# A two-layer attention kernel: one PSUM bank per head for scores and exponentials, whole sums per key tile, preparation without a bank of its own

## The chip, the cores and the metric

The kernel runs on one core of a Trainium2 chip. The metric is the device time of one execution in microseconds; the time before is the median of three runs. The engines are named as the profile names them: PE is TensorE's matmul stream and PEld its weight loads, DVE is VectorE, ACT is ScalarE, POOL is GpSimd, SP is SyncE, which here issues DMAs.

## The reference, cut to what matters

The input is 2048 tokens of 256 features. Two transformer layers follow each other, each an attention and an MLP with the same MLP weights. The first attention has 16 query heads, 4 key heads, biases and rotary positions; the second has 16 of each and neither biases nor rotation.

```
scores = einsum("bthd,bshd->bhts", q, k) * scale      # head size 16
scores = where(causal, scores, -inf)
probs  = softmax(scores, axis=-1)                     # maximum, exponential, sum, division
x = x + einsum("bhts,bshd->bthd", probs, v).reshape(B, S, 256) @ Wo.T + bo
x = x + ((tanh-gelu of (n @ Wg.T)) * (n @ Wu.T)) @ Wd.T      # n = layernorm(x), 2048 features
```

Everything is 32-bit floating point; the MLP weights arrive as 4-bit codes with scales.

## The kernel before, in words

The tokens are cut into 4 blocks of 512 queries (`NB`, `TB`), each of 4 tiles of 128 (`NT`). A unit of attention is one block b and one group g of four heads, 16 units per layer, run in order by `Attention.run` (L848). A unit has nk = 4(b+1) key tiles of 128 keys, and each key tile has two steps, one for each pair of heads (p = 0, 1).

For every query the maximum over its keys is needed before the exponentials. `max_steps` (L659) makes it for the next unit: a maxima step writes the scores of 128 queries against up to 512 keys for two heads (L670) into a pair of PSUM banks, and DVE reduces both banks at once (L682). At the end `gather` and `turn` (L711, L717) put the negated maxima, as three bf16 parts, into `mT`.

`value_steps` (L724) makes the current unit. `pair` (L750) writes, for two heads r = 0, 1, the negated maxima by a bf16 matmul (L758) and on top of them keys times queries (L763) into one pair of banks, and ACT takes one exponential over both banks (L775) into a buffer `e` (four of them). `values` (L729) multiplies the exponentials of the key tile before with the values, four heads side by side in 32 output columns of the array each (L743), and adds into the bank `av`. It is called twice for a key tile, after each pair, for half of the queries each time; where 256 queries or fewer are left (the last two of the four diagonal key tiles) the first call does all. The 17th column of the values is one, so that the same sum gives the softmax's divisor. `end` copies the sums out (L790), `divide` turns and divides them (L797 to L807).

On diagonal key tiles a mask is added by small matmuls (`add_mask`, L639). This and the reading that follows it are put on a list (`owed`) and done when `settle` (L650) is next called: by the next `pair` or `values`, or, if a maxima mask is on the list, by the next maxima step.

The order on every engine is written out by hand: `weave` (L42) puts side steps between main steps evenly, so that after each pair's scores come the maxima steps of the next unit and the preparation of the next block (norms, turns, projections) and, in the first attention, of the unpacking of the MLP weights, and then the sums (the second part of a step's tuple). The first three steps of a unit take maxima only, the last three take no side steps. In the last unit of a layer there are no maxima. `cut` and `holding` (L67, L74) keep a preparation whose scores bank is still to be read (`plain`, `high`, L539, L543) from being split between units.

PSUM has eight banks. `ps_s` (L121) hands out three pairs of banks in turn, to maxima steps and to exponential pairs alike, and to `features` in the MLP (L930); `ps_av` is one bank, and `ps_m` (L127) is one bank for everything else: turns of the input (L464), projections (L498), values (L565), turned maxima (L711), division (L797), output projection (L837), the MLP's turns (L910) and half of its second product (L959). A buffer that is handed out again makes PE wait for the engine that read it last.

In the second attention a projection is split into a high part that ACT rounds (L545) and a rest that DVE subtracts (L553); both go to DRAM by DMAs that SP issues (L552, L556) and come back in other layouts as `qT` (SP, L631) and `kT` (GpSimd's queue, L618).

## Time and profile before

| what | value |
|---|---|
| time, median of 3 runs | 1888.08 us (1885.3 to 1889.78) |
| the profiled execution's own time | 1890.76 us |
| its span | 1888.9 us |
| PE busy | 1766.7 us, 94% |
| DVE busy | 1123.3 us, 59% |
| ACT busy | 805.2 us, 43% |
| POOL busy | 239.0 us, 13% |
| mean granted clock of TensorE | 0.982 |

The profile is of one execution. Busy time of PE is not time at its peak: matmuls overlap, and their ends are modelled. In a timeline a row is a run of equal instructions on one engine, with start and duration in us; a bracket tells how long the engine sat idle before it and which engine's instruction ended that. In a group row come line, engine, operation, output and inputs by name, shapes, count, then busy us, mean ns of one, and idle time with its releasers. A 32-bit matmul appears as two records, its two passes. PE's groups of attention are L758, L763, L670, L743 and the masks L645; the MLP's are L934 and L959.

### The profile page before, as it was taken

What the parts mean: (1) busy time and instruction counts of PE and PEld (TensorE: products, weight loads), DVE (VectorE), ACT (ScalarE), POOL (GpSimd) and SP (SyncE); (2) the same over time, 40 slices, a digit from 0 to 9 for tenths busy, and PEclk for the clock granted to TensorE, in tenths of its full rate; (3) what the DMA queues carried; (4) which work ended last, traced back from release to release, by engine and by line L of the source; (5) the groups of instructions that cost most, each with busy time, mean ns of one, the idle gap of its engine ahead of it and who ended that gap; (6) DMA issues with size and microseconds to landing.
All of it is one profiled execution on the core that took longest, in us unless ns stands there. A gap on an engine that the chain in (4) does not pass through costs nothing. (4 is left out here: it accounts for less than half of the span.)

```text
span 1888.9 us, 31839 instructions
## 1 busy us (share of the span) xinstructions
PE 1766.7 (94%) x13452; PEld 928.5 (49%) x13452; DVE 1123.3 (59%) x1676; ACT 805.2 (43%) x1069; POOL 239.0 (13%) x437
## 2 busy tenths in 40 slices
PE   5788889999999999999998898999999999999999
PEld 3344444444444456656564444444444444756656
DVE  4567687778786253544445667766877715363442
ACT  1334455555667531222213355556566662131221
POOL 4111321210001011112101010010000001011110
PEclk8889999999999999999998999999999999999999
DMA  4421310310101100001303232041000010000000
GB/s 100 108 60 37 68 52 23 63 35 24 35 24 35 45 6 1 1 0 42 81 1 74 62 72 54 12 90 33 15 13 2 2 46 1 11 1 11 7 6 12
DMA packets 42271, 64.24 MB, mean 34 GB/s; under 512 B 13840, under 2 KB 20880, under 8 KB 41872
## 3 DMA queue, kind: packets, MB, share of 16 engines
q1 hardware_dynamic: 33488, 45.93, 8.2%
q0 software_dynamic: 7680, 15.74, 5.0%
q8 instruction: 106, 1.74, 0.4%
q10 hardware_dynamic: 960, 0.52, 0.1%
q14 instruction: 37, 0.30, 0.1%
HBM read 44.24 MB, written 17.83 MB: 33 GB/s over the span
## 5 line engine op out<-in xcount | busy, mean ns | idle before, releaser
L682 DVE TENSOR_REDUCE mx<-ps_s 128x2 f32<-128x1024 f32 (+3 forms) x640 | 658.2, 1060 | 221.0 <-PE ps_s L645 116.0
L775 ACT ACTIVATE e<-ps_s 128x1024 f32<-128x1024 f32 (+3 forms) x640 | 571.3, 897 | 422.6 <-PE ps_s L763 244.8
L743 PE MATMUL ps_av<-e,v 128*32 128x256 f32 (+1 forms) x4608 | 365.2, 384 | 3.4 <-ACT e L775 3.4
L763 PE MATMUL ps_s<-qT,kT 64*128 64x512 f32 (+3 forms) x1280 | 341.7, 527 | 0.0
L670 PE MATMUL ps_s<-kT,qT 64*128 64x512 f32 (+3 forms) x1280 | 269.2, 423 | 52.3 <-DVE mx L682 22.8
L758 PE MATMUL ps_s<-mT,sel 64*128 64x512 bf16 (+3 forms) x1280 | 232.7, 358 | 27.3 <-ACT mT L717 10.1
L934 PE MATMUL ps_s<-xnT,wg 128*128 128x512 f32 x512 | 242.1, 595 | 0.0
L934 PE MATMUL ps_s<-xnT,wu 128*128 128x512 f32 x512 | 240.6, 592 | 0.0
L670 PEld LDWEIGHTS ps_s<-kT,qT 64*128 64x128 f32 x1280 | 130.1, 188 | 161.6 <-ACT e L775 66.5
L758 PEld LDWEIGHTS <-sel 64*128 64x128 bf16 x1280 | 75.0, 93 | 251.2 <-issue 242.3
L942 DVE TENSOR_TENSOR t<-ps_s,t 128x512 f32<-128x512 f32 x128 | 88.1, 688 | 164.5 <-POOL t L941 162.7
L940 ACT ACTIVATE t<-ps_s 128x512 f32<-128x512 f32 x128 | 76.2, 595 | 251.8 <-PE ps_s L934 251.3
L943 ACT ACTIVATE t<-t 128x512 f32<-128x512 f32 x128 | 80.6, 629 | 200.7 <-DVE t L942 200.7
L934 PEld LDWEIGHTS ps_s<-xnT,wu 128*128 128x128 f32 x512 | 97.3, 190 | 122.7 <-issue 122.7
L941 POOL TENSOR_SCALAR t<-t 128x512 f32<-128x512 f32 x128 | 79.1, 618 | 573.0 <-ACT t L940 572.5
L743 PEld LDWEIGHTS ps_av<-e,v 128*32 128x32 f32 x4608 | 95.0, 108 | 109.1 <-issue 89.5
L934 PEld LDWEIGHTS ps_s<-xnT,wg 128*128 128x128 f32 x512 | 96.0, 192 | 106.0 <-issue 104.0
L944 DVE SCALAR_TENSOR_TENSOR t<-t,ps_s 128x512 f32<-128x512 f32 x128 | 88.0, 688 | 89.0 <-ACT t L943 89.0
L763 PEld LDWEIGHTS ps_s<-qT,kT 64*128 64x128 f32 x1280 | 130.5, 199 | 0.0
L959 PE MATMUL ps_m<-wd,inter 128*128 128x256 f32 x512 | 114.5, 380 | 0.0
L959 PE MATMUL ps_av<-wd,inter 128*128 128x256 f32 x512 | 114.5, 380 | 0.0
L959 PEld LDWEIGHTS ps_av<-wd,inter 128*128 128x128 f32 x512 | 96.7, 190 | 17.1 <-issue 4.5
(125 smaller groups left out, 1179.9 us busy)
## 6 DMA issues: line engine op xcount, KB each, us to landing
qT<-h SPq DMA_DIRECT2D x256, 64.0 KB, 2.2
kT<-h POOLq DMA_DIRECT2D x96, 128.0 KB, 5.9
h<-high SPq DMA_DIRECT2D x24, 256.0 KB, 2.6
h<-low SPq DMA_DIRECT2D x24, 256.0 KB, 2.5
wd<-wd_kept SPq DMA_DIRECT2D x2, 2048.0 KB, 7.8
wd_kept<-dq_d SPq DMA_DIRECT2D x4, 512.0 KB, 2.7
out<-x SPq DMA_DIRECT2D x16, 128.0 KB, 1.7
x<-x SPq DMA_DIRECT2D x3, 512.0 KB, 5.4
```

Source lines behind the costliest of these rows:

```text
L670: nc.tensor.matmul(pt[:, r, :w], lhsT=self.qT[b, g][64 * r : 64 * r + 64, p, i * P : (i + 1) * P], rhs=self.key_rows(c, g, p, r, slice(0, w)),
L682: nc.vector.tensor_reduce(held["mx"][:, i, 2 * p : 2 * p + 2, c], pt[:, :, :w], AX.X, ALU.max)
L743: nc.tensor.matmul(held["av"][32 * j : 32 * j + 32, own], lhsT=self.vv[kt // NT][:, kt % NT, h * VW : h * VW + 32], rhs=es_[j // 2][:, j % ...
L758: nc.tensor.matmul(pt[:, r, q0:], lhsT=sel[64 * r : 64 * r + 64, p, :], rhs=self.mT[b, g][64 * r : 64 * r + 64, q0:], start=True, stop=False,)
L763: nc.tensor.matmul(pt[:, r, q0:], lhsT=self.key_rows(kt // NT, g, p, r, keys), rhs=self.qT[b, g][64 * r : 64 * r + 64, p, q0:], start=Fals ...
L775: nc.scalar.activation(e[:, :, q0:], pt[:, :, q0:], AF.Exp, scale=QK_SCALE)
L934: nc.tensor.matmul(pt[:, k, :], lhsT=w[:, c, fc * P : (fc + 1) * P], rhs=self.xnT[b][:, c, :], start=(c == 0), stop=(c == 1),)
L941: nc.gpsimd.tensor_scalar(t, t, GELU_A, 1.0, ALU.mult, ALU.add)
L942: nc.vector.tensor_tensor(t, gate, t, ALU.mult)
L943: nc.scalar.activation(t, t, AF.Tanh, scale=GELU_C)
L944: nc.vector.scalar_tensor_tensor(t, t, 1.0, gate, ALU.add, ALU.mult)
L959: nc.tensor.matmul(po[:, :D], lhsT=inter[:, fc, i * P : (i + 1) * P], rhs=wd[:, fc, :], start=(fc == 0), stop=(fc == NFC - 1),)
```

## The change

It shares the eight banks out anew: two pairs (`ps_s`) for maxima, three single banks (`ps_e`) of which a pair takes two, one for each head, and `ps_av`. The bank `m` is gone: inside an attention's `run`, `ps_m` settles owed maxima masks and takes a maxima pair (using half of it); elsewhere it takes a single bank. The exponential of a pair becomes two, one per head. `values` is called once for a key tile, after its second pair, over all queries. The plain projection in the second attention is rounded and copied out at once (ACT, DVE), and its rest is subtracted by GpSimd from the copy; so the holding back of cuts goes. In the MLP every third feature step uses two single banks in place of a pair. The core of the diff:

```diff
@@ -62,18 +62,6 @@
     keyed = [((n + 0.5) / len(a), 0, n, f) for n, f in enumerate(a)]
     keyed += [((n + 0.5) / len(b), 1, n, f) for n, f in enumerate(b)]
     return [f for *_, f in sorted(keyed, key=lambda k: k[:3])]
-def cut(steps, n):
-    while 0 < n < len(steps) and getattr(steps[n - 1], "open", False):
-        n += 1
-    return steps[:n], steps[n:]
-def holding(f):
-    f.open = True
-    return f
 @with_exitstack
@@ -118,14 +106,25 @@
     psum = ctx.enter_context(tc.tile_pool(name="psum", bufs=1, space=PSUM))
     dram = ctx.enter_context(tc.tile_pool(name="dram", bufs=1, space=bass.MemoryType.DRAM))
     def ps_s():
-        return psum.tile([P, 2, 512], F32, tag="s", name="ps_s", bufs=3)
+        return psum.tile([P, 2, 512], F32, tag="s", name="ps_s", bufs=2)
+    def ps_e():
+        return psum.tile([P, 512], F32, tag="e", name="ps_e", bufs=3)
     def ps_av():
         return psum.tile([P, 512], F32, tag="av", name="ps_av")
+    owner = {"at": None}
     def ps_m():
-        return psum.tile([P, 512], F32, tag="m", name="ps_m")
+        if owner["at"] is None:
+            return ps_e()
+        owner["at"].settle("max")
+        return ps_s()[:, 0, :]
     xt = [const.tile([P, NT, D], F32, tag=f"x{b}", name=f"x{b}") for b in range(NB)]
@@ -539,6 +538,13 @@
             def plain(c, n):
                 held["of"] = room(c, 0)
                 project(held["of"], wqkv, c, n)
+                if alone:
+                    return
+                high(c, n)
+                r = self.wk.tile([P, TB], F32, tag="r0", name="r", bufs=1)
+                nc.vector.tensor_copy(r[:n], held["of"][:n])
+                held["of"] = r
             def high(c, n):
                 h = pre.tile([P, TB], F32R, tag="high", name="high", bufs=2)
@@ -550,9 +556,8 @@
                 h = held["high"]
                 lo = pre.tile([P, TB], F32R, tag="low", name="low", bufs=2)
                 nc.sync.dma_start(out=to[0], in_=h[:n].bitcast(F32))
-                nc.vector.tensor_tensor(
-                    lo[:n], held["of"][:n], h[:n].bitcast(F32), ALU.subtract
-                )
+                by = nc.vector if first or alone else nc.gpsimd
+                by.tensor_tensor(lo[:n], held["of"][:n], h[:n].bitcast(F32), ALU.subtract)
                 nc.sync.dma_start(out=to[1], in_=lo[:n].bitcast(F32))
                 (self.q_d if c < 2 else self.k_d)[b, c] = to
@@ -593,8 +598,9 @@
                 elif first:
                     steps += [lambda c=c, n=n, s=s: rotated(c, n, s) for s in range(2)]
                 else:
-                    steps.append(holding(lambda c=c, n=n: plain(c, n)))
-                steps += [holding(lambda c=c, n=n: high(c, n)), lambda c=c, n=n: low(c, n)]
+                    steps.append(lambda c=c, n=n: plain(c, n))
+                steps += [lambda c=c, n=n: high(c, n)] if first or alone else []
+                steps.append(lambda c=c, n=n: low(c, n))
                 if c >= 2:
                     steps.append(lambda c=c: self.load_k(b, c))
                 elif c == 0 and load:
@@ -643,7 +649,7 @@
                 for r in range(2):
                     rows = slice(64 * r, 64 * r + 64)
                     nc.tensor.matmul(
-                        pt[:, r, to], lhsT=mask_w[rows, kind, part, :],
+                        pt[r][:, to], lhsT=mask_w[rows, kind, part, :],
                         rhs=mask_t[rows, kind, part, :], start=False, stop=(part == 1),
                     )
@@ -675,7 +681,7 @@
                     )
                 def masked():
-                    self.add_mask(pt, 0, w - P)
+                    self.add_mask([pt[:, r, :] for r in range(2)], 0, w - P)
                     reduced()
                 def reduced():
@@ -726,25 +732,18 @@
             nk = NT * (b + 1)
             held = {"pending": []}
-            def values(half):
+            def values():
                 self.settle()
-                kt, q0, es_ = held["pending"][0]
-                few = TB - q0 <= TB // 2
-                if half == 1:
-                    held["pending"].pop(0)
-                    if few:
-                        return
-                elif kt == 0:
+                kt, q0, es_ = held["pending"].pop(0)
+                if kt == 0:
                     held["av"] = ps_av()
-                own = slice(q0, TB) if few else slice(*((q0, TB // 2), (TB // 2, TB))[half])
                 for j in range(4):
                     h = g if self.first else 4 * g + j
                     nc.tensor.matmul(
-                        held["av"][32 * j : 32 * j + 32, own],
+                        held["av"][32 * j : 32 * j + 32, q0:],
                         lhsT=self.vv[kt // NT][:, kt % NT, h * VW : h * VW + 32],
-                        rhs=es_[j // 2][:, j % 2, own],
-                        start=(kt == 0 and half == 0), stop=(kt == nk - 1),
+                        rhs=es_[j // 2][:, j % 2, q0:], start=(kt == 0), stop=(kt == nk - 1),
                     )
             def pair(kt, p):
@@ -752,16 +751,16 @@
                 diagonal = kt >= NT * b
                 keys = slice((kt % NT) * P, (kt % NT + 1) * P)
                 self.settle()
-                pt = ps_s()
+                pt = [ps_e(), ps_e()]
                 for r in range(2):
                     nc.tensor.matmul(
-                        pt[:, r, q0:], lhsT=sel[64 * r : 64 * r + 64, p, :],
+                        pt[r][:, q0:], lhsT=sel[64 * r : 64 * r + 64, p, :],
                         rhs=self.mT[b, g][64 * r : 64 * r + 64, q0:], start=True, stop=False,
                     )
                 for r in range(2):
                     nc.tensor.matmul(
-                        pt[:, r, q0:], lhsT=self.key_rows(kt // NT, g, p, r, keys),
+                        pt[r][:, q0:], lhsT=self.key_rows(kt // NT, g, p, r, keys),
                         rhs=self.qT[b, g][64 * r : 64 * r + 64, p, q0:],
                         start=False, stop=not diagonal,
                     )
@@ -772,7 +771,10 @@
                     exponentials()
                 def exponentials():
-                    nc.scalar.activation(e[:, :, q0:], pt[:, :, q0:], AF.Exp, scale=QK_SCALE)
+                    for r in range(2):
+                        nc.scalar.activation(
+                            e[:, r, q0:], pt[r][:, q0:], AF.Exp, scale=QK_SCALE
+                        )
                 if diagonal:
                     self.owed.append(("exp", masked))
@@ -784,8 +786,7 @@
                     held["pending"].append((kt, q0, held["es"] + [e]))
             def end():
-                values(0)
-                values(1)
+                values()
                 o = pre.tile([P, TB], F32, tag="o", name="o")
                 nc.scalar.copy(o, held["av"])
                 held["o"] = o
@@ -811,7 +812,7 @@
             for kt in range(nk):
                 for p in range(2):
                     scored = lambda kt=kt, p=p: pair(kt, p)
-                    steps.append((scored, lambda p=p: values(p)) if kt else scored)
+                    steps.append((scored, values) if kt and p else scored)
             return steps, end, divide
         def out_steps(self, b):
@@ -848,6 +849,7 @@
         def run(self, extra, beside):
+            owner["at"] = self
             units = [(b, g) for b in range(NB) for g in range(NG)]
             per_unit = -(-len(extra) // (len(units) - NG))
             ending, ahead = [], []
@@ -858,12 +860,11 @@
                 if g == 0 and b + 1 < NB:
                     ahead = self.prep_steps(b + 1)
-                    few = -(-(len(ahead) - (7 if self.first else 5)) // 2)
+                    few = -(-(len(ahead) - (7 if self.first else 4)) // 2)
                 if n >= NG:
                     more, extra = more + extra[:per_unit], extra[per_unit:]
                 if g < 3:
-                    part, ahead = cut(ahead, few)
-                    more += part
+                    more, ahead = more + ahead[:few], ahead[few:]
                 if n + 2 < len(units):
                     self.load_q(*units[n + 2])
                 maxima, turn = [], None
@@ -884,6 +885,7 @@
                 weave(steps[3:], blend(maxima[first:], more) if maxima else more, rest=3)
                 ending = [end, divide]
             end()
+            owner["at"] = None
             return [divide] + [lambda: None] * 2 + self.out_steps(NB - 1)
@@ -928,14 +930,16 @@
                     inter = ff.tile([P, NFC, TB], F32, tag="inter", name="inter", bufs=1)
                     def features(fc, b=b, inter=inter):
-                        pt = ps_s()
+                        pt = [ps_e(), ps_e()] if fc % 3 == 2 else ps_s()
+                        pt = pt if fc % 3 == 2 else [pt[:, k, :] for k in range(2)]
                         for k, w in ((0, wg), (1, wu)):
                             for c in range(2):
                                 nc.tensor.matmul(
-                                    pt[:, k, :], lhsT=w[:, c, fc * P : (fc + 1) * P],
+                                    pt[k], lhsT=w[:, c, fc * P : (fc + 1) * P],
                                     rhs=self.xnT[b][:, c, :], start=(c == 0), stop=(c == 1),
                                 )
-                        gate, up = pt[:, 0, :], pt[:, 1, :]
+                        gate, up = pt
                         t = ff.tile([P, TB], F32, tag="t", name="t", bufs=3)
                         nc.scalar.activation(t, gate, AF.Square)
                         nc.gpsimd.tensor_scalar(t, t, GELU_A, 1.0, ALU.mult, ALU.add)
```

## The prediction

> **What bounds the kernel now.** I read the page's engine totals first, then the timeline of one unit (a query block and four heads) of block 3 in the second attention, then the groups by shape, then the granted clock by stretch.
>
> ```profile
> span 1888.9 us, 31839 instructions
> PE 1766.7 (94%) x13452; PEld 928.5 (49%) x13452; DVE 1123.3 (59%) x1676; ACT 805.2 (43%) x1069; POOL 239.0 (13%) x437
> ```
>
> PE is the engine that is nearly always occupied. The attentions take about 60 to 600 and 940 to 1540 us, the rest is MLP. In the timeline below (start, duration, engine, line) the unit from 1410.1 to 1456.5 us runs at its regular pace:
>
> ```profile
> 1421.02 0.39 PE L758 MATMUL ps_s<-mT,sel 64*128 64x512 bf16 x2
> 1421.06 0.58 PE L763 MATMUL ps_s<-qT,kT 64*128 64x512 f32 x2
> ...
> 1421.48 0.39 PE L670 MATMUL ps_s<-kT,qT 64*128 64x512 f32 x2
> 1421.74 1.02 ACT L775 ACTIVATE e<-ps_s 128x1024 f32<-128x1024 f32 x1 [0.42 <-PE ps_s L763]
> ...
> 1421.81 0.64 PE L743 MATMUL ps_av<-e,v 128*32 128x256 f32 x8
> ...
> 1422.38 0.39 PE L758 MATMUL ps_s<-mT,sel 64*128 64x512 bf16 x2
> ...
> 1423.24 0.64 PE L743 MATMUL ps_av<-e,v 128*32 128x256 f32 x8
> ...
> 1423.82 0.39 PE L758 MATMUL ps_s<-mT,sel 64*128 64x512 bf16 x2
> ```
>
> Read starts, not durations, since ends overlap. One step is a pair of heads: scores (L758, L763) 0.46 us until the maxima step L670, that 0.33 until the sums L743, those 0.57 until the next scores: 1.36, the measured step. The next is 1.44, so a key tile (two steps) takes 2.80 us. ACT starts its exponential 0.72 us after L758 starts, and is covered: the buffer it holds is asked for three allocations later. PE sets the pace.
>
> The last unit of a layer has no maxima left:
>
> ```profile
> 1522.11 0.39 PE L758 MATMUL ps_s<-mT,sel 64*128 64x512 bf16 x2
> ...
> 1523.35 0.39 PE L758 MATMUL ps_s<-mT,sel 64*128 64x512 bf16 x2
> ...
> 1524.47 0.39 PE L758 MATMUL ps_s<-mT,sel 64*128 64x512 bf16 x2
> ```
>
> Here the tile takes 1.24 + 1.12 = 2.36 us.
>
> **What the sums give back.** A half sum of 256 columns costs 0.57 us and about 0.11 of the step from L670 (0.33 less the 0.22 a pass of 512 columns takes), each switch between 64-row and 128-row weights showing up as a gap. One sum of 512 columns has the same two passes, each 0.213 us longer: 0.57 + 0.43 = 1.00. Two halves with their gaps are 1.36, one whole 1.11: 0.25 us less per key tile. The split is undone at 256 of the 320 key tiles (the two narrow diagonal ones of each of 32 units were never split), so 64 us of PE work and switches go.
>
> **What the new buffers ask for.** Three single banks serve pairs that need two each. The built order of the changed kernel shows what this means: the second head's L758 of every pair waits for the first head's exponential of the pair just before. The order is pair 0, maxima, pair 1, maxima, sums, so the pair-0-to-pair-1 gap has no sum in it. Behind this wait stand, in order on PE, both key matmuls, the maxima and the sums.
>
> ```profile
> L775 ACT ACTIVATE e<-ps_s 128x1024 f32<-128x1024 f32 x448 | 457.1, 1026 | 311.8 <-PE ps_s L763 244.8 <-PE ps_s L645 63.4 <-PE ps_s L670 0.8
> L775 ACT ACTIVATE e<-ps_s 128x512 f32<-128x512 f32 x64 | 38.0, 597 | 38.2 <-PE ps_s L645 38.0
> ```
>
> An exponential of 512 columns takes 597 ns by this row. From L758 of pair 0: 0.72 until ACT starts, 0.60, and 0.05 from ACT's end to PE's start (where PE waits for ACT in this trace): pair 1 can start its second head at 1.37, where PE would be there at 0.46 + 0.22 = 0.68. So 0.69 us of wait, and then 0.46 + 0.33 + 1.00: a tile of 3.16 us for 2.80, **+0.36**. With no maxima: 1.37 + 0.43 + 0.11 + 1.00 = 2.91 to 2.93 for 2.36, **+0.57**. Where the gap has a second maxima step or a preparation (0.24 to 1.9 us of PE), that work moves into the wait: 3.16 for about 3.1 to 3.2, **0**, or up to -0.25. From pair 1 to the next pair 0 the sum of 1.00 covers the release.
>
> ACT's own load: by the rows, splitting costs 2 x 597 - 1026 = 168 ns per pair, 4 x 0.597 = 2.39 us per tile. The Trainium skill (ScalarE: Activation LUTs, What ACT_TABLE_LOAD costs) gives 186 ns plus 0.833 ns per column and an overlap of 93 ns between back-to-back ACTIVATEs, an estimate of 2.08 us per tile. By either ACT stays under 2.93, so it is no bound; what hurts is the latency of the first one, to which the overlap gives nothing. With the overlap I lose nothing of the sum, without it ACT has 20% left.
>
> **Per unit.**
> - First two tiles. Before 1.21 + 1.03 + 2.56 + 1.79 = 6.6 us. After, pair (1,0) also waits on (0,1), with the copy of the finished sums (0.58) ahead of that exponential on ACT; following the releases I get 6.5: **0**. In the last unit 4.9 becomes 6.5: +1.6.
> - Four diagonal tiles. Their mask is owed until pair 1 settles it, so the exponential starts only there. Waits after the mask: 0.34 + width (597, 491, 386, 278 by shape; the last two rows and the fit of 168 + 0.84 per column). Tiles of 3.24, 3.29, 1.75 and 1.99 us become about 3.6, 3.4, 2.2 and 2.75 (in the last one, the mT copy of 585 ns goes ahead on ACT): **+1.7**.
> - Block 3, middle units: nine plain tiles, of which the built order covers one and lengthens another: 26.4 to 28.7, +2.3, plus 1.7: **+4.0** each (two per layer). The unit with the output projection: +3.3. The last: 1.6 + 10 x 0.57 + 1.0 = +8.3. Together 19.6.
> - Block 2: eight plain tiles, about half covered by second maxima and preparations, one preparation standing before the owed mask, where it covers nothing (0.9): +4.0 three times. The fourth unit carries 32 maxima on 24 pairs, about 35.7 us of DVE in 39.8: DVE paces it, +0.7. Together 12.7.
> - Block 1: 2.7 three times and 1.0: 9.1. Block 0, all diagonal and full of preparations: 1.5 each, 6.
>
> A layer sums to 47. In the first one PE is busy 181.4 of 200 us between 200 and 400, against 190.6 in 1200 to 1400, so part of its PE waits for others and can swallow the new wait: 0.8 of it. 38 + 47 = **85**.
>
> **The other edits.** Preparations (some 150 allocations: turns, divisions, projections) move from their own bank into the two maxima slots, so the maxima behind wait for their readers on DVE or, after the exponentials, on ACT. PEld's waits in L670 today average 0.4 us (126.5 us in 304 waits, mostly beside running matmuls). Bounds: -7 (PE's own waits for the old single bank) to +45 (0.3 each); as most have a microsecond or more between, I take +3. The second attention's plain projections add 12 DVE copies for 12 subtractions (0.69 for 0.68: nothing) and 12 GpSimd subtractions; the nearest row, L518, has 1.27 us: 15 us on an engine busy 9 of 200 us, ahead of the key loads issued from that queue (8 issues of 0.52). Keys are used in a later unit: 0; uncovered, at most 12 x 0.6 = 7. The moved boundaries of preparations are in the order used above. MLP: every third feature step takes two single banks: PE is busy 217 of 220 us between 640 and 860 and the distance between uses stays three: 0, bounds -2 to +3. Start-up with two slots for three: 0 to +2.
>
> **The clock.** The stalls could gate it. The Trainium skill (TensorE: Matmul & The Clock Gate, Why this matters for your kernels) warns only of idle gaps over about 3 us. This trace is stricter (columns: stretch, its length, busy PE, PEld, DVE, ACT, POOL, granted clock, DMA):
>
> ```profile
> 128.50:131.90 3.40, 2.19 (x36) 1.49 (x36) 3.19 (x6) 0.81 (x1) 0.00 (x0) 1.00 0.00 0
> 131.90:138.70 6.80, 6.77 (x76) 3.68 (x72) 5.74 (x11) 1.50 (x3) 0.00 (x0) 0.50 0.00 0
> ```
>
> A stretch 64% busy is followed by 6.8 us at half clock, and no idle gap of PE around it is longer than 1.3 us. By the rule the new waits cost nothing more. By the row, tiles with 0.69 idle in 3.16 (about 80%) keep the clock, but unit starts (1.8 idle in 4.5) may lose some: from 0 to 32 units x 1.7 us = 54 (half of one such window each). I take the side of the 80% tiles and put this in the range.
>
> **Sum.** 85 + 3 = 88. The profiled execution took 1890.8 us (span 1888.9 and 1.9 around it); 1978.8 after. The median of the runs lies 2.7 lower: **1976 us**.
>
> **Rivals.**
> 1. DVE absorbs it. Units are DVE-paced more often than I count: then only block 3, the diagonals and the last units pay, about 15 to 60 us: 1905 to 1950. For it: DVE is busy 36.7 of 46.5 us in the unit shown. Against: PE waits there for DVE almost never. Chance 0.14.
> 2. The clock gate follows the waits: 1976 + 54 = 2030, over 2013. Chance 0.12.
> 3. Faster. One mechanism: whole sums free 0.25 us per tile, 64 us, and the maxima's own slots free PE of waits on ACT. It decides where the mean uncovered wait per tile is under 0.25, which needs an exponential to release its bank within about 0.9 us of L758, or most gaps to be covered. With 40 us of diagonal and end waits left it would give 1888 - 64 + 40 = 1864. Against: 0.72 + 0.60 + 0.05 in the trace, and an order that does put the wait there. Chance 0.08, and 0.02 for a draw.
> 4. Bound by ACT: 2.39 per tile is below every tile's new time; it adds nothing.
>
> The main case (1950 to 2013) has 0.64. Slower by over 0.2% (which is about what a measurement can tell from no change): 0.90; within: 0.02; faster: 0.08. The range 1915 to 2025 leaves out the gain and most of the clock case.
>
> **What would show it.** In the changed profile: L758's matmuls waiting for ACT's exponential as PE's largest wait, 0.5 to 0.7 us some 200 times; key tiles of 3.1 to 3.2 us at regular pace and 2.9 in the last unit; PE's busy share down to some 86 to 90%; fewer, longer sums (2 x 512 columns, 1.0 us to the next scores); exponentials of 597 ns, ACT about 110 us busier; MLP stretches unchanged. I am wrong if tiles stay at 2.8 us, or if maxima waiting for preparation readers, not scores for exponentials, lead the waits.

## The result, and the profile after

The changed kernel takes 1989.22 us (median of 4 runs, 1986.31 to 1993.78), the kernel before on the same chip 1888.93 us (4 runs): a ratio of 1.0534 [1.0511, 1.0557]. The prediction was 1976 us in a range of 1915 to 2025. The profiled execution took 1986.31 us, its span is 1984.5, the granted clock 0.973 for 0.982.

The engine totals of the changed kernel, to be read against those of before:

```profile
span 1984.5 us, 28451 instructions
PE 1779.4 (90%) x11404; PEld 903.3 (46%) x11404; DVE 1126.1 (57%) x1676; ACT 843.9 (43%) x1709; POOL 254.2 (13%) x449
```

PE has 2048 records fewer (the half sums) and is busy 13 us longer, in a span 96 us longer. So most of the loss is PE standing still. The list of what PE waits for names the place (columns: engine, output and line, releaser; us in total, times, the longest):

```profile
PE ps_e L757 <- ACT e L775: 95.7, 211, 3.3
PE ps_s L676 <- DVE mx L688: 34.1, 92, 0.9
```

L757 is the former L758, the matmul that opens a head's bank, and L676 the former L670. The same list before, its longest entry and that of the scores for an exponential:

```profile
PE ps_s L670 <- DVE mx L682: 22.8, 47, 1.2
PE ps_s L758 <- ACT e L775: 4.5, 16, 0.4
```

That 95.7 us of these waits stand beside a growth of 96 us is chance: the list counts idle time from modelled ends, so a real wait is longer (see below), and the whole sums give time back. One key tile at regular pace, from the timeline of the second attention's block 3:

```profile
1499.48 0.39 PE L757 MATMUL ps_e<-mT,sel 64*128 64x512 bf16 x2
...
1500.17 0.39 PE L757 MATMUL ps_e<-mT,sel 64*128 64x512 bf16 x1
1500.20 1.08 ACT L775 ACTIVATE e<-ps_e 128x512 f32<-128x512 f32 x2 [0.80 <-PE ps_e L762]
...
1500.84 0.37 PE L757 MATMUL ps_e<-mT,sel 64*128 64x512 bf16 x1 [0.29 <-ACT e L775]
...
1501.61 1.07 PE L743 MATMUL ps_av<-e,v 128*32 128x512 f32 x8
...
1502.61 0.39 PE L757 MATMUL ps_e<-mT,sel 64*128 64x512 bf16 x2
```

Pair 1's first head starts at 1500.17, its second only at 1500.84, released by ACT: 1.36 us after pair 0's start at 1499.48 (L757, L762 and L676 leave one record per head, only the sums two). The first exponential starts at 1500.20, 0.72 after L757. The tile is 1499.48 to 1502.61, 3.13 us. The bracket shows 0.29 of idle, not 0.67, because the first head's matmul is drawn as running until 1500.56. In the last unit, without maxima:

```profile
1601.73 0.39 PE L757 MATMUL ps_e<-mT,sel 64*128 64x512 bf16 x2
1602.19 0.39 PE L757 MATMUL ps_e<-mT,sel 64*128 64x512 bf16 x1
1603.08 0.37 PE L757 MATMUL ps_e<-mT,sel 64*128 64x512 bf16 x1 [0.51 <-ACT e L775]
1604.61 0.39 PE L757 MATMUL ps_e<-mT,sel 64*128 64x512 bf16 x2
```

The second head again comes 1.35 us after the pair before it started, and the tile takes 2.88 (mean over the unit 2.89 to 2.90).

Cut at the starts of the blocks' first scores, and at an attention's end at the start of its last pair's scores, the two traces differ as follows (us; the growth beside the prediction's):

| stretch | before, 1st attention | after | before, 2nd attention | after | growth, 1st + 2nd | predicted |
|---|---|---|---|---|---|---|
| block 0 | 87.7 | 95.0 | 75.0 | 87.2 | 7.3 + 12.2 | 4.8 + 6 |
| block 1 | 135.3 | 141.5 | 121.0 | 132.2 | 6.2 + 11.2 | 7.3 + 9.1 |
| block 2 | 175.2 | 184.1 | 164.3 | 176.0 | 8.9 + 11.7 | 10.2 + 12.7 |
| block 3 | 183.0 | 202.4 | 182.3 | 201.4 | 19.4 + 19.1 | 15.7 + 19.6 |
| start, MLPs, end | 765.1 | 764.7 | | | -0.4 | 0 |

From the unrounded starts the attentions grow by 41.7 and 54.3 us (38 and 47 predicted, and 3 more for the preparations in slots, somewhere in them), the rest by nothing. The last row also holds the tail of each last unit, which grows by 0.6 to 0.7 us. The profiles are single executions: run 3 below leaves the first attention as it is, yet its blocks 0, 1 and 2 there differ from the changed kernel's by +1.9, -1.3 and +2.2 us, so differences of that size in these blocks say nothing. Block 3 repeats to some 0.3 us.

### The profile page after: what moved, and what is told of

The parts are those of the page before. It is cut to its first block, busy times and chain, and to the rows that moved or that the text cites. A ratio compares the mean times of both kernels' runs of the same rounds, so it can differ in the third digit from the quotient of the medians.

```text
span 1984.5 us, 28451 instructions
## 1 busy us (share of the span) xinstructions
PE 1779.4 (90%) x11404; PEld 903.3 (46%) x11404; DVE 1126.1 (57%) x1676; ACT 843.9 (43%) x1709; POOL 254.2 (13%) x449
## 4 chain that ended last, share of the span: by engine, by line
PE 68%; DVE 12%; issue 8%; ACT 7%; DMA 2%; POOL 2%; SPq 0%; ACTq 0%; DVEq 0%; POOLq 0%
PE ps_s L938 15%; PE ps_av L743 11%; DVE mx L688 9%; PE ps_e L757 7%; PE ps_e L938 7%; ACT e L775 6%; PE ps_e L963 6%; PE ps_av L963 5%; PE ps_e L762 5%; PE ps_s L676 4%; PE ps_s L497 3%; PE ps_s L570 1%; DMA h<-low 1%; POOL kT L624 1%; PE ps_s L838 1%
## 5 line engine op out<-in xcount | busy, mean ns | idle before, releaser
L688 DVE TENSOR_REDUCE mx<-ps_s 128x2 f32<-128x1024 f32 (+3 forms) x640 | 663.0, 1062 | 268.4 <-PE ps_s L676 140.1
L775 ACT ACTIVATE e<-ps_e 128x512 f32<-128x512 f32 (+3 forms) x1280 | 613.9, 532 | 445.5 <-PE ps_e L762 251.6
L757 PE MATMUL ps_e<-mT,sel 64*128 64x512 bf16 (+3 forms) x1280 | 321.8, 357 | 99.4 <-ACT e L775 95.7
L762 PE MATMUL ps_e<-qT,kT 64*128 64x512 f32 (+3 forms) x1280 | 347.2, 518 | 0.0
L676 PE MATMUL ps_s<-kT,qT 64*128 64x512 f32 (+3 forms) x1280 | 276.9, 414 | 54.7 <-DVE mx L688 34.1
L743 PE MATMUL ps_av<-e,v 128*32 128x512 f32 (+3 forms) x2560 | 308.4, 555 | 0.0
L676 PEld LDWEIGHTS ps_s<-kT,qT 64*128 64x128 f32 x1280 | 146.3, 195 | 139.9 <-DVE mx L688 86.3
L762 PEld LDWEIGHTS ps_e<-qT,kT 64*128 64x128 f32 x1280 | 127.0, 195 | 165.7 <-issue 163.4
L757 PEld LDWEIGHTS <-sel 64*128 64x128 bf16 x1280 | 64.8, 94 | 282.0 <-issue 279.7
L938 PE MATMUL ps_s<-xnT,wg 128*128 128x512 f32 x352 | 165.7, 593 | 0.0
L938 PE MATMUL ps_s<-xnT,wu 128*128 128x512 f32 x352 | 165.4, 592 | 0.0
L963 PE MATMUL ps_e<-wd,inter 128*128 128x256 f32 x512 | 114.5, 380 | 0.0
L963 PEld LDWEIGHTS ps_e<-wd,inter 128*128 128x128 f32 x512 | 96.9, 190 | 14.3 <-issue 1.1
L938 PEld LDWEIGHTS ps_s<-xnT,wg 128*128 128x128 f32 x352 | 65.3, 191 | 70.6 <-issue 67.8
```

What stands on the lines that cost most here:

```text
L676: nc.tensor.matmul(pt[:, r, :w], lhsT=self.qT[b, g][64 * r : 64 * r + 64, p, i * P : (i + 1) * P], rhs=self.key_rows(c, g, p, r, slice(0, w)),
L688: nc.vector.tensor_reduce(held["mx"][:, i, 2 * p : 2 * p + 2, c], pt[:, :, :w], AX.X, ALU.max)
L743: nc.tensor.matmul(held["av"][32 * j : 32 * j + 32, q0:], lhsT=self.vv[kt // NT][:, kt % NT, h * VW : h * VW + 32], rhs=es_[j // 2][:, j % ...
L757: nc.tensor.matmul(pt[r][:, q0:], lhsT=sel[64 * r : 64 * r + 64, p, :], rhs=self.mT[b, g][64 * r : 64 * r + 64, q0:], start=True, stop=False,)
L762: nc.tensor.matmul(pt[r][:, q0:], lhsT=self.key_rows(kt // NT, g, p, r, keys), rhs=self.qT[b, g][64 * r : 64 * r + 64, p, q0:], start=Fals ...
L775: nc.scalar.activation(e[:, r, q0:], pt[r][:, q0:], AF.Exp, scale=QK_SCALE)
```

## The experiments

In the comparisons "old banks" are those of before (three pairs for maxima and exponentials alike, one exponential per pair). "New banks" stands for the whole rest of the change: the single banks, and with them two exponentials per pair, preparations in the maxima slots, GpSimd's subtraction and the new sharing in the MLP.

**1 and 2: the two halves of the change.** The first takes the changed kernel and gives it back the half sums, the second takes the kernel before and gives it the whole sums.

```diff
 first, on the changed kernel (values(half) as before):
-                    steps.append((scored, values) if kt and p else scored)
+                    steps.append((scored, lambda p=p: values(p)) if kt else scored)
 second, on the kernel before (values() as after):
-                    steps.append((scored, lambda p=p: values(p)) if kt else scored)
+                    steps.append((scored, values) if kt and p else scored)
```

> The changed kernel with the sums cut in halves again, one after each pair; its banks, split exponentials and preparation in the maxima slots stay. Theory (each pair waits for the exponential of the pair just before, and the whole sums took the cover out of the gap): a step is 0.46 scores, 0.33 maxima, 0.57 half sum = 1.36 us, and the exponential's release comes at 1.37, so the wait all but goes; a key tile of block 3 takes 2.75 to 2.8 us for 3.12, and PE's waits of scores for exponentials fall from 96 us to under 25. Time 1880 to 1905. Rival (preparations in the maxima slots, or twice as many exponentials on ACT, cost the time): both are still there, 1945 to 1990.

> The kernel before with one part of the change alone: whole sums, once for a key tile after its second pair; three pairs of banks, one exponential for a pair and the bank for preparation stay. Theory: without a half sum in the gap the second maxima step of a tile gets the pair of banks of the exponential three allocations back, which is free 0.72 + 1.02 + 0.05 = 1.79 us after that pair's scores began, where PE arrives at 1.14; a tile is 1.79 + 0.22 + 0.11 + 1.00 = 3.12 us for 2.80, as in the changed kernel, but in the last unit, without maxima, about 2.1 to 2.3 for 2.36. Time 1945 to 1975. Rival (the new sharing of the banks is what costs, whole sums are a pure gain of 0.25 us at 256 tiles): 1825 to 1870.

New banks with half sums: 1917.39 us, 1.016 [1.0142, 1.0178]. Old banks with whole sums: 1906.93 us, 1.0099 [1.0077, 1.012]. Neither hit its interval: the first is above the theory's and below the rival's, the second between both. Together they say more than either expectation:

| | half sums | whole sums |
|---|---|---|
| old banks | 1889 | 1907 (+18) |
| new banks | 1917 (+28) | 1989 (+100) |

18 + 28 is 46; the other 54 us exist only where both are together. With new banks and half sums the gap between pair 0 and pair 1 holds half a sum. The second head still starts 1.36 us after the pair before, but now PE has as much work until then: steps of 1.36, tiles of 2.72 us in block 3, and in that kernel's waits (L764 and L782 are the same two lines) the wait for ACT shrinks to a fifth:

```profile
PE ps_s L676 <- DVE mx L688: 35.7, 75, 1.2
PE ps_e L764 <- ACT e L782: 20.5, 39, 3.1
```

The second kernel's waits show what whole sums do to the old banks (L751 and L768 are its L757 and L775):

```profile
PE ps_s L670 <- ACT e L768: 48.2, 99, 1.2
PE ps_s L751 <- ACT e L768: 27.3, 45, 1.0
```

There the maxima stand behind the exponential of the pair before, in a tile of 3.23 us at full pace. But tiles without maxima fall to 2.00 us (0.46 + 1.54), and its last unit takes 32.2 us for 37.8 before. The whole loss is small: blocks 0 to 2 lose 8 us in the first attention and 7 in the second, block 3 loses 2.0 in each.

**3: the GpSimd subtraction put back on DVE.**

```diff
-                by = nc.vector if first or alone else nc.gpsimd
+                by = nc.vector
```

> The changed kernel with the rest of the projections subtracted by VectorE in place of GpSimd. Theory of a small side cost (at 1076 to 1082 us in the changed kernel, GpSimd issues key loads that wait for a DMA, the subtraction stands behind them, the copy on DVE waits 6.9 us for it and a maxima step on PE 2.7, followed by half clock): 6 to 12 us faster, 1977 to 1984, all of it in block 0 and 1 of the second attention, whose block 0 shrinks from 87.2 to about 79 us. If GpSimd is off the path everywhere, as the prediction had it: 1987 to 1991.

1982.49 us, 1.0496 [1.0478, 1.0513]: 6.7 us less than the changed kernel by the medians, inside the first interval. The timeline of the changed kernel shows one place that this edit touches, in block 0 of the second attention:

```profile
1077.06 3.03 POOL L624 DMA_DIRECT2D kT<-h  x6 [3.78 <-DMA h<-low]
1080.09 1.27 POOL L560 TENSOR_TENSOR low<-r,high 128x512 fp32r<-128x512 f32 x1
1081.40 0.69 DVE L546 COPY r<-ps_s 128x512 f32<-128x512 f32 x1 [6.87 <-POOL low L560]
1082.15 0.33 PE L676 MATMUL ps_s<-kT,qT 64*128 64x128 f32 x2 [2.74 <-DVE r L546]
```

The key loads that GpSimd issues wait for the rest to land in DRAM (3.78 us, then six issues of 0.5). The next subtraction stands behind them on the same queue, the copy into the single buffer `r` waits for it on DVE (6.87), and PE waits for the copy (2.74). In run 3 DVE no longer waits for a subtraction on GpSimd, and PE's waits of maxima for `r` fall from 4.9 to 2.0 us. But block 0 of the second attention shrinks only to 84.4 us, where I expected about 79, and block 1 by 1.1; the two profiled executions differ by 0.4 us in all. So the direction is clear by the medians, and where all of the 6.7 us were is not shown.

**4: the sums after the first pair instead of the second.**

```diff
-                    steps.append((scored, values) if kt and p else scored)
+                    steps.append((scored, values) if kt and not p else scored)
...
```

A second hunk adapts the last step of a unit, which now has no sums, to the turn of the maxima that is put into it.

> The changed kernel with the whole sum of the key tile before placed after the first pair instead of after the second. Theory: the wait belongs to whichever gap has no sum, as every pair needs a bank of the pair just before; it moves from the gap between pair 0 and 1 to the one between pair 1 and the next pair 0, and stays 0.69 us a tile: tiles of 3.1 to 3.2 us, 1975 to 2000. Rival (it is only the place of the sums, whose 1.0 us could cover the exponential if it stood in the right gap): 1890 to 1930.

1996.26 us, 1.0571 [1.0554, 1.0587]; waits of L757 for ACT 86.9 us, 203 times, tiles of 3.12 and 2.90 as in the changed kernel. The sum covers whichever gap it is in, and the other one waits.

**5 and 6: two other parts, alone on the kernel before.** The first puts the preparations into the slots of the maxima and copies the plain projections out at once; the second splits the exponential per head, on the old pair of banks.

```diff
 first:
-        return psum.tile([P, 512], F32, tag="m", name="ps_m")
+        if owner["at"] is None:
+            return psum.tile([P, 512], F32, tag="m", name="ps_m")
+        owner["at"].settle("max")
+        return ps_s()[:, 0, :]
...
 second:
-                    nc.scalar.activation(e[:, :, q0:], pt[:, :, q0:], AF.Exp, scale=QK_SCALE)
+                    for r in range(2):
+                        nc.scalar.activation(
+                            e[:, r, q0:], pt[:, r, q0:], AF.Exp, scale=QK_SCALE
+                        )
```

> The kernel before, with the preparation of an attention moved from its own bank into the pairs that maxima and exponentials share, as in the change (projections of the second attention rounded and copied out at once, but the rest subtracted by VectorE); sums in halves, three pairs, one exponential for a pair. The two runs with one half of the change each left about 20 us unexplained in block 0 of both attentions (97.3 and 85.1 us with the new banks and half sums, against 87.7 and 75.0). If the maxima waiting for the readers of preparations make them: block 0 grows by 5 to 10 us in each attention and the rest by 1 to 3 a block, 1898 to 1915. If the exponentials' banks or GpSimd make them: 1886 to 1893.

> The kernel before with one edit: each pair's exponential is issued as two, one for a head, on the old pair of banks. ACT gets about 40 us busier by the changed kernel's page (844 for 805). Theory (ACT has room, only the release matters, which here comes 0.1 us later than with one exponential): 1887 to 1896. Rival (the load on ACT costs): 1900 to 1920.

Preparations in slots: 1898.26 us, 1.0062 [1.0043, 1.0081]. The time is at the edge of what I expected, but not for my reason: block 0 did not grow (89.0 and 73.0 us); blocks 1 and 2 of the first attention did, by 2.4 and 3.0, those of the second by 0.8 and 2.0, which is hardly more than two executions differ by. Split exponentials: 1899.74 us, 1.0074 [1.0057, 1.009], so 12 us more than the kernel before (1888.17 in that comparison), where my theory had at most 8. Two exponentials take 1.08 us for the 1.02 of one over both banks, the pair is released that much later, and block 3 pays 3.0 and 3.1 us, in steps of 1.86 for 1.79 and 1.29 for 1.24.

**7: the second head's exponential first.**

```diff
                 def exponentials():
-                    for r in range(2):
+                    for r in (1, 0):
```

> The changed kernel with the two exponentials of a pair issued in the other order, the second head's first. The bank that the next pair's second head needs is then released by the later one, 0.49 us later by the changed kernel's timeline (1.08 us for two). If the wait for that release sets the tile, a tile of block 3 goes from 3.12 to 3.6 us, 0.48 at some 200 to 240 gaps: 2075 to 2105. If the time lies in the shared slots or on ACT's load, 1985 to 2000.

1989.57 us, 1.0541 [1.0525, 1.0557], no change, where I expected 90 to 120 us more. That lies in the interval of shared slots or ACT's load, but it does not speak for them: in its trace the second head starts 1.37 us after the pair before, not 0.49 later than in the changed kernel, and the waits for ACT are 97.8 us, 212 times. The built order tells why: banks are handed out in the order in which they come free, so the second head of the next pair still waits for the exponential that was issued first. The edit did not lengthen the wait, so this run says nothing about its price.

**8: whole sums only where there are no maxima**, on the kernel before: in the last two key tiles of a unit and in a layer's last unit.

```diff
-                    steps.append((scored, lambda p=p: values(p)) if kt else scored)
+                    if not last and kt < nk - 2:
+                        steps.append((scored, lambda p=p: values(p)) if kt else scored)
+                    else:
+                        steps.append((scored, lambda: values(None)) if kt and p else scored)
...
```

> The kernel before with whole sums only where no maxima step stands between the pairs: the last two key tiles of every unit, and all of a layer's last unit; banks, exponentials and preparation as before. From the run with whole sums everywhere on the old banks: last units 5.6 us shorter each, and the four last steps of a unit 3.07 us for 3.74: 11 + 32 x 0.3 to 0.65 = 20 to 32 us faster, 1857 to 1870. If the gain of those stretches depends on whole sums elsewhere: 1880 to 1890.

1875.87 us, 0.9938 [0.9923, 0.9953]: faster than both kernels, by less than expected. Its last units gain the 5.6 us each (32.2 for 37.8), since a tile there falls from 2.36 to 2.01:

```profile
1497.91 0.39 PE L758 MATMUL ps_s<-mT,sel 64*128 64x512 bf16 x2
1498.38 0.39 PE L758 MATMUL ps_s<-mT,sel 64*128 64x512 bf16 x2
1498.92 1.06 PE L743 MATMUL ps_av<-e,v 128*32 128x512 f32 x8
1499.92 0.39 PE L758 MATMUL ps_s<-mT,sel 64*128 64x512 bf16 x2
```

The other units of block 3 gain 0.2 to 0.4 us each. Thirty such gains and the two last units would be some 20 us; the medians show 12, the two profiled executions 15, and where the rest went is not shown.

**9: four single banks.** The changed kernel with four single banks for exponentials, one pair for maxima, and again a bank for preparation.

```diff
-        return psum.tile([P, 2, 512], F32, tag="s", name="ps_s", bufs=2)
+        return psum.tile([P, 2, 512], F32, tag="s", name="ps_s", bufs=1)
...
-        return psum.tile([P, 512], F32, tag="e", name="ps_e", bufs=3)
+        return psum.tile([P, 512], F32, tag="e", name="ps_e", bufs=4)
...
-        if owner["at"] is None:
-            return ps_e()
-        owner["at"].settle("max")
-        return ps_s()[:, 0, :]
+        return psum.tile([P, 512], F32, tag="m", name="ps_m")
...
```

In the MLP two of every three feature steps now take single banks.

> The changed kernel with four single banks for exponentials, one pair for maxima and a bank of its own for preparation (2 + 4 + 1 + 1 = 8). My theory (three single banks for pairs that take two make the second head wait for the exponential just before): with four, a bank is asked for again two pairs later, so the wait of the second head's L757 (here L754) for ACT falls from 95.7 us to under 25, and the last unit of a layer, which has no maxima, falls from 44.6 to 32-34 us (tiles of 2.9 to about 2.0). But the maxima, two per key tile in one pair of banks, now each wait for the reduction before (score 0.45, DVE 1.2 us): tiles with maxima 3.3 to 3.5 for 3.12, PE's largest wait is L673 for DVE, well over 100 us. Total 1990 to 2060. Rival (the wait is due to split exponentials or to whole sums, whatever the number of banks): last unit stays at 43 to 46 us and the wait for ACT stays near 95.

2296.75 us, 1.216 [1.212, 1.2201]. The total missed upwards, for two reasons. One pair for the maxima costs more than I derived: tiles at regular pace in block 3 are 3.65 us (0.74 + 2.91), where I had at most 3.5, and others take 3.9 to 7.1, some of them at half clock. And the granted clock, which I had left out, is 0.901 over the whole run, for 0.973; if stretches scale with it, that is up to some 170 us more than in the changed kernel, an estimate from its mean in each block. Block 2 of the first attention in the changed kernel, and then in run 9 (length; busy PE, PEld, DVE, ACT, POOL; clock; DMA share and GB/s):

```profile
288.50:472.60 184.10, 161.63 (x1350) 70.59 (x1348) 137.24 (x192) 101.78 (x209) 31.31 (x54) 0.99 0.16 36
357.70:597.20 239.50, 187.20 (x1348) 75.96 (x1344) 142.12 (x192) 100.00 (x211) 31.18 (x54) 0.84 0.12 28
```

What the run was for came out: the wait of the scores for an exponential is gone (the group's only idle time is 1.3 us, for another reason), and PE waits for DVE instead. Its group of scores and its largest wait (L754, L673 and L685 are L757, L676 and L688):

```profile
L754 PE MATMUL ps_e<-mT,sel 64*128 64x512 bf16 (+3 forms) x1280 | 261.4, 390 | 1.3 <-ACT mT L720 1.3
```

```profile
PE ps_s L673 <- DVE mx L685: 344.0, 386, 2.2
```

Its last unit, which has no maxima, takes 34.1 us for 44.6, in tiles of 2.00 and 2.35 in turn:

```profile
1924.67 0.39 PE L754 MATMUL ps_e<-mT,sel 64*128 64x512 bf16 x2
...
1924.92 4.08 ACT L772 ACTIVATE e<-ps_e 128x512 f32<-128x512 f32 x8 [0.28 <-PE ps_e L759]
...
1926.23 0.39 PE L754 MATMUL ps_e<-mT,sel 64*128 64x512 bf16 x2
1926.69 0.73 PE L754 MATMUL ps_e<-mT,sel 64*128 64x512 bf16 x2
...
1928.57 0.39 PE L754 MATMUL ps_e<-mT,sel 64*128 64x512 bf16 x2
```

The split exponentials and the whole sums are still there, so the cause of the wait is the number of single banks, not those two as such. The rival of this run has fallen.

**10: both maxima of a tile put into the gap that waits.** On the changed kernel, the side steps after pair 1 move to after pair 0.

```diff
-        want = min(len(side), -(-(n + 1) * len(side) // max(1, len(main) - rest)))
+        want = min(len(side), -(-(n + 1 + ahead * (n % 2)) * len(side) // max(1, len(main) - rest)))
...
-                weave(steps[3:], blend(maxima[first:], more) if maxima else more, rest=3)
+                weave(steps[3:], blend(maxima[first:], more) if maxima else more, rest=3, ahead=1)
```

> The changed kernel with both side steps (maxima) of a key tile placed between pair 0 and pair 1, where the second head waits, none between pair 1 and the sums. My theory (the wait is a fixed latency of 1.36 us from the first head's scores, and other work put into it is free): the second head of pair 1 still starts 1.36 us after pair 0's first, now with two maxima steps ahead of it, and the other half of the tile loses one maxima of 0.33: tile 3.12 to about 2.8 where both reductions keep up, over some 120 plain tiles with maxima; the last units (no maxima) stay at 44 to 45. Total 1945 to 1970. Rival (PE's own work sets the tile, the wait only stands beside it; or the two maxima in a row wait for DVE): tile stays 3.1 or more, total 1980 to 2020.

2014.53 us, 1.0675 [1.0656, 1.0693]: the time went with the rival. Tile by tile it is both. The timeline of a unit of block 3 has a tile with two maxima and then one with three:

```profile
1579.79 0.39 PE L757 MATMUL ps_e<-mT,sel 64*128 64x512 bf16 x2
...
1580.25 0.62 PE L676 MATMUL ps_s<-kT,qT 64*128 64x512 f32 x4
...
1580.72 0.81 PE L757 MATMUL ps_e<-mT,sel 64*128 64x512 bf16 x2
...
1582.68 0.39 PE L757 MATMUL ps_e<-mT,sel 64*128 64x512 bf16 x2
...
1584.87 0.50 PE L676 MATMUL ps_s<-kT,qT 64*128 64x512 f32 x2 [1.09 <-DVE mx L688]
...
1586.75 0.39 PE L757 MATMUL ps_e<-mT,sel 64*128 64x512 bf16 x2
```

With two maxima in the gap the tile is 2.89 us for 3.12: the wait took in one of them, as the theory says. With three, the third finds both pairs of banks still being reduced and waits for DVE: 4.07. In block 3's middle units this nets to about -1 us each; blocks 1 and 2, with more side steps per tile, grow by 5.4 to 11.7 us over the changed kernel. I had left the uneven spread of the side steps out of the expectation.

## Why the prediction was right, step by step

**The wait.** Its three terms were 0.72 + 0.60 + 0.05 = 1.37 us; measured 1.36. Tiles: 3.16 predicted, 3.12 to 3.13 measured; without maxima 2.91 to 2.93, measured 2.88 to 2.90. It was to be PE's largest wait, some 200 times: it is, 211 times (0.45 us each by the list, which counts less than the 0.67 between the starts). Run 4 moves it, run 9 removes it, run 10 fills it, and by runs 1 and 2 whole sums cost 72 us on the new banks for 18 on the old. That it comes from three single banks for pairs that take two is shown by run 9.

**The sum of units.** Block 3 of the second attention was to grow by 3.3 + 4.0 + 4.0 + 8.3; it grew by 4.1 + 4.2 + 3.9 + 7.5, the last unit followed to the copy of its sums (6.8 to the table's cut). That the sums are so near is in part luck. In the middle units the first two tiles, taken at 0, grew by 0.5, the nine plain ones by 2.4 and 2.6 (2.3 predicted), the diagonal ones by 1.0 and 1.1 (1.7). In the last unit the start, taken at +1.6, grew by 0.7, the ten plain tiles by 5.5 (5.7), the diagonal ones by 1.3 (1.0). The units of block 2, taken at 4.0 three times and 0.7, grew by 2.1, 5.9, 1.0 and 2.6. The factor of 0.8 for the first attention, the least founded step, gave 38 for 41.7. By the medians the kernel grew by 100 us for 88; nearly 9 of these 12 are block 0's.

**What the whole sum gives back.** 0.25 us per tile were taken. Without maxima it is 0.35 (2.36 to 2.01 in run 8). I had priced one switch between weight shapes, and two go there; that this is the difference is argued, not shown. In tiles with maxima no run shows it by itself, since the old banks then wait (run 2).

**Where sizes were off.**
- The GpSimd subtraction: "uncovered, at most 12 x 0.6 = 7", taken at 0. Run 3 gives 6.7. The bound was right in size, but not for its reason: the trace shows one wait of 6.87 us on DVE, of which PE feels 2.74, not twelve small ones. The step I failed to follow is that the key loads ahead of the next subtraction themselves wait for a DMA.
- Block 0: 10.8 predicted, 19.5 measured. The stretches' rows (length; busy PE, PEld, DVE, ACT, POOL; granted clock; DMA share and GB/s) for the first and the second attention, of before:

```profile
52.40:140.10 87.70, 72.23 (x734) 38.25 (x734) 52.80 (x92) 29.75 (x46) 17.09 (x26) 0.86 0.32 70
998.20:1073.20 75.00, 63.26 (x718) 34.84 (x719) 46.08 (x83) 29.93 (x47) 9.19 (x17) 0.93 0.34 78
```

and of the changed kernel:

```profile
52.00:147.00 95.00, 76.16 (x668) 40.97 (x667) 53.60 (x92) 31.48 (x78) 17.10 (x26) 0.79 0.29 64
1038.10:1125.30 87.20, 66.47 (x653) 35.98 (x653) 46.26 (x83) 32.10 (x79) 14.20 (x21) 0.87 0.29 68
```

In the first attention length times clock is 75.4 before and 75.0 after: the lower clock is large enough to explain the growth there. In the second it is 69.8 and 75.9, so the clock leaves some 6 us to waits, run 3's among them. If a stretch scales wholly with its clock, the drops are worth 7.7 and 5.6 us in the two block 0s. Elsewhere it moves little: 0.99 to 0.97 and 0.98 in block 1, 1.00 to 0.99 in block 2, 1.00 in block 3 as before. Summed over both attentions, length times the missing part of the clock goes from some 20 to some 41 us. So at most some 20 us of the growth are the clock's, an estimate from these windows: more than the 0 that the prediction took, less than the rival's 54, and up to 8 of them lie in blocks 1 and 2, where the waits then account for less than they seem to. Every kernel with new banks is longer in the first attention's block 0 (94 to 103 us, run 9 113) than those with old banks (86 to 89), and length times clock there is 72 to 76 in all of them but run 9 (79): they differ there by their clock. Which part of the new banks lowers it is open: the preparations in slots and the split exponentials do not lengthen the block, each by itself.
- The clock's rule. The prediction read from one row that a stretch 64% busy loses the clock and one 80% busy keeps it. Other rows of the same trace of before don't fit: 79% busy was followed by half clock, 61% was not.

```profile
111.40:114.80 3.40, 2.69 (x36) 2.09 (x35) 3.16 (x7) 0.60 (x1) 3.40 (x7) 1.00 0.50 168
114.80:118.30 3.50, 3.50 (x41) 1.41 (x34) 2.22 (x7) 0.98 (x2) 2.34 (x5) 0.51 0.21 66
159.70:163.10 3.40, 2.07 (x36) 1.15 (x28) 3.24 (x10) 1.39 (x2) 0.00 (x0) 1.00 0.01 2
163.10:166.50 3.40, 3.23 (x52) 1.44 (x44) 3.00 (x9) 1.19 (x2) 1.10 (x2) 1.00 0.00 0
```

That the tiles with the new wait keep their clock came true in block 3, but one row was too little ground for it.
- Preparations in slots: +3 taken, inside bounds of -7 to +45; run 5 gives +10 on the old banks. Split exponentials cost 12 there, which the prediction had not priced on their own. Their sum with GpSimd's 7 is 29, about all of run 1's 28, but they are not its parts one by one: run 1 lost in block 0 (9.6 and 10.2 us), and these two did not.
- ACT: "about 110 us busier"; it is 38.7. Here the row, at 2.39 us per tile, was the worse guide: one exponential alone takes 0.60, but two in a row 1.08 and eight 4.08 (run 9), 0.51 each or 2.04 per tile. The estimate from the Trainium skill's page (ScalarE: Activation LUTs, What ACT_TABLE_LOAD costs), 2.08 with its overlap, fits that. ACT is no bound in the changed kernel, as both had it; in run 9's last unit, where the wait is gone, the tiles average 2.17, close to two such pairs of 1.08, and ACT is busy 15.15 of 16.00 us.

**The rivals.** DVE did not absorb the wait in blocks 1 and 2, which grew by 38 us for the 39.3 predicted, though unevenly and with the clock's part in it. The clock rival came true in part, in block 0. The faster case would have needed an exponential to release its bank 0.9 us after L757; it took 1.36.

## What to carry to other kernels

Ask of every buffer pool how many allocations lie between two uses of a buffer and how long its reader takes from the first write: three single banks for requests of two put the second head one pair after its reader, and a fixed latency of 1.36 us landed in a gap with 0.68 us of work. The two halves of this change cost 18 and 28 us alone and 100 together, since half a sum in each gap had been the cover of the wait; price a change's parts together, and look for the part that is worth having where its cover isn't needed (whole sums where no maxima run: 12 us faster). Before moving work to a queue that also issues DMAs, see what those DMAs wait for.

## What was not expected of the hardware

- Exponentials of 512 columns take 0.60 us alone, 1.08 for two in a row and 4.08 for eight: the time of one is not the load of many, and the load of many is not the latency of one.
- The granted clock in block 0 fell from 0.86 to 0.79 although PE's records there are busy for 80 to 82% of the stretch in both kernels. In block 3, with a stall in every tile, it stays at 1.00. In run 9, with more of short waits (PE busy for 78% of block 2, no idle gap in the attentions over 2.2 us), it falls to 0.84 there. No long gap is needed for that, and the busy share alone does not tell when it happens. What does is open.
- A sum over 512 columns where two of 256 stood saves 0.35 us, although the same columns pass through the array.
